# Conditioned graph attention: a re-ordered set-up, with batch 0's feature transform in seven block products

## The chip, the core and the metric

The kernel runs on one core of a Trainium2 chip. Its engines work in parallel, each through its own queue, in order: TensorE (PE in the profile, with its weight loads as PEld), VectorE (DVE), ScalarE (ACT), GpSimd (POOL) and SyncE (SP), which here only issues DMAs. They meet through semaphores. The metric is the device time of one execution in microseconds; lower is better. All arithmetic is float32 unless it is said otherwise.

## The reference

For 16 batches of 512 nodes with 512 features, a query vector is joined to every node (to nodes whose features sum to zero, a zero vector), and `self_feat = [x, q] @ W_self.T + b_self` follows. Twice, with an adjacency tensor and with its transposed form, 16-head attention over the first 20 nodes is added:

```python
vcq = concatenate([exp_v, where(row_zero, 0.0, q)], axis=-1)
self_feat = vcq @ W_self.T + b_self
output = self_feat
for d in range(2):
    A = (adj if d == 0 else swapaxes(adj, 1, 2))[:, :, :20, :]
    cond, vb = A.sum(-1), A @ w_bias + b_bias
    # heads of 32 features; keys and values are rows 0..19 of self_feat
    aff = einsum(q_heads, k_heads) / sqrt(32)
    aff = where(cond > 0, aff, -9e15) + vb
    output += grouped_output(softmax(aff) @ self_feat[:, :20])
return x + relu(output)
```

`x` is 16x512x512, the query 16x512, the label tensor 16x512x512x11 (int32), `W_self` 512x1024, and the query, key and output weights are two sets of 512x512.

## The kernel before, in words

Features lie on the 128 partitions in four chunks (C = 4) and nodes along the free dimension, halved and with the 20 key nodes put first in each half. A float32 matmul shows as two records in the trace. Several small matmuls run side by side in different parts of TensorE's array (`HA`, `HL` count such parts).

The work has two stages. The **set-up** is common to all batches; the **loop** does the 16 batches, software-pipelined over several periods, in an order written out by hand in the strings `order` and `moved`. The set-up too is issued in the order of the program text (`manual_schedule`), so that each engine's queue holds its instructions in that order.

The set-up goes through these steps:

- Loads of the 320 key-node columns (`xkv`), the feature half of `W_self` (`ws_v`) and the query half (`ws_q`), while seven warm-up matmuls run (L591).
- `kv_terms` (L646): the key nodes' features against `ws_v`, by chunk k of the contraction.
- The query's contribution `qw` (L656 to L671) and the flags `nzk` of key nodes with a non-zero sum (L663, L664); both are multiplied into `qp` (L681: one of the four by VectorE, three by GpSimd) and added into `kvT` (L686) and `kvn` (L690).
- `row_sums(0)` (L191, L193): GpSimd adds up batch 0's rows when `x` has landed, for the row flags. `row_flags` (L200, L203) counts with TensorE and stores the flags to DRAM, from where `load_nz` brings them back on all partitions.
- Eight `key_rows` (L703; copied out by L709 on ScalarE and L710 on VectorE), four of them ahead of the first burst and one ahead of each of bursts 1 to 4.
- Twenty bursts of `keys` (L800), n = 0 to 19: key rows against query weights, into two pairs of PSUM banks. ScalarE copies out one pair (L821) and VectorE the other (L823). The next burst writes the same banks. The finished groups go to DRAM (L826, four stage buffers).
- With bursts 0 to 3 VectorE also runs two `bias_terms` each (L719: a product of `wq_sb` and `br_sb`, both in SBUF, with an accumulated sum). From burst 4 on, the string `plan` names what else is issued behind each burst: `b` is `biases` (L725 to L731 on VectorE), `v` and `w` value matmuls (L769, copied out by L775, stored by L777), `n` and `l` the row flags and their loads, `c` the bias scores, `s` a step of batch 0's `self_feat`. At fixed bursts stand `weight_differences` (L787), the masks of batch 0 (`first_mask_mul`, `_count`, `_sum`: L337, L354, L357, L362) and, at burst 12, `weight_sums` (L241 to L244, GpSimd).

Batches 1 to 15 get their `self_feat` in the loop by seven block products of the 2x2 block matrices of weights and nodes, instead of eight (`feature_product`, L292). For that GpSimd forms sums of weight blocks once (`weight_sums`) and four differences of node blocks per batch (`x_sum`, L266). The products gather in two PSUM banks, `ps_u` and `ps_v`, and the copies in between (`feature_copy`, `feature_second`, `feature_third`, `feature_join`) add the query's part. Batch 0 is made directly: `self_feat` (L220), 16 matmuls for each of four blocks, three blocks in the set-up and the last at the entry of the loop, with `self_copy` (L232).

At the entry of the loop GpSimd forms sums of keys and features (`key_sum` L401, `self_sum` L411). The first of them writes memory that the set-up's pool held, so it waits for that pool's last users. The matmuls of the scores are L428 (`P1` to `P7`); `P6` needs `key_sum(0, 2)` and `self_sum(0, 2)`.

Of the kernel before, what the change touches and what calls it, by code (L numbers as in the profile page):

```python
# [8 lines left out]
I32 = mybir.dt.int32  # L9
AF = mybir.ActivationFunctionType  # L10
# [8 lines left out]
def gat_kernel(  # L19
# [68 lines left out]
    qw = const.tile([P, C, B], F32, name="qw")  # L88
# [4 lines left out]
    qd = const.tile([P, 2, B], F32, name="qd")  # L93
# [10 lines left out]
    wts, outs, held, sf_ps, conds, prods, both = {}, {}, [None] * 3, {}, {}, {}, {}  # L104
    sums, us, soft_w, diffs, held_sums = {}, {}, {}, {}, {}
# [105 lines left out]
    def self_feat(b, f, h, parts, to=None):  # L211

        for i, ks in parts:
            if (i, ks[0]) == (0, 0):
                if (f, h) == (0, 0):
                    new_self(b)
                held[0] = bank(f"ps_sf{b}_{f}{h}") if to is None else to
            for k in ks:
                for a in range(HA):
                    nc.tensor.matmul(  # L220
                        held[0][bass.ts(a, RA), bass.ds(i * HN, HN)],
                        ws_v[:, k, bass.ds((2 * f + i) * P + a * RA, RA)], xs[b][:, k, half(h)],
                        start=(i, k) == (0, 0), stop=k == C - 1, skip_group_check=True,
                    )
            if (i, ks[-1]) == (1, C - 1):
                sf_ps[b, f, h] = held[0]

    def self_copy(b, f, h):

        ps = sf_ps.pop((b, f, h))  # L230
        for i in range(2):
            nc.vector.scalar_tensor_tensor(  # L232
                sfs[b][:, 2 * f + i, half(h)], nzs[b][:, half(h)], qw[:, 2 * f + i, b : b + 1],
                ps[:, bass.ts(i, HN)], ALU.mult, ALU.add,
            )

# [20 lines left out]
    def x_sum(b, n):  # L257

        t = sums[b, n] = xsum.tile([P, 2, HN], F32, tag=f"t{n}", name=f"t{b}_{n}")
# [6 lines left out]
        nc.gpsimd.tensor_sub(t, one, two)  # L266

    def side(t):
        return t[:, : 2 * HN].rearrange("p (i n) -> p i n", i=2)

    def feature_product(b, n):
# [12 lines left out]
        for i in range(2):  # L284
            for k in range(2):
                for a in range(HA):
# [3 lines left out]
                    else:  # L290
# [3 lines left out]
                        start=(n, i, k) == (1, 0, 0), stop=k == 1, skip_group_check=True,  # L294
                    )

# [254 lines left out]
    with tc.tile_pool(name="setup", bufs=1) as sp, tc.tile_pool(  # L551
# [7 lines left out]
        sel = sp.tile([P, B], F32, name="sel")  # L559
# [12 lines left out]
        with tc.tile_pool(name="setup_k", bufs=1) as sk:  # L572
# [6 lines left out]
            nc.vector.memset(ps_q[:, 0], 0.0)  # L579
            nc.vector.memset(bqbd, 0.0)  # L580
            nc.gpsimd.memset(zero, 0.0)

            nc.gpsimd.memset(sel, 0.0)
            for k in range(C):
                nc.gpsimd.affine_select(
                    out=sel, in_=sel, pattern=[[-1, B]], compare_op=ALU.not_equal, fill=1.0,
                    base=-k * DH, channel_multiplier=1,
                )
# [22 lines left out]
            for k in range(3):  # L611
# [42 lines left out]

            for k in range(C):
                nc.tensor.matmul(  # L656
                    ps_q[bass.ds(k * DH, B), 0], q_sb[:, k], ws_q[:, k], start=True, stop=True
                )
            q4 = sk.tile([P, F], F32, name="q4")
            nc.scalar.copy(q4, ps_q[:, 0])  # L660
            ps = ps_s.tile([P, 2, 512], F32, tag="s", name="ps_q")
            counts = ps[:, 1, P : P + BM]
            nc.tensor.matmul(counts, ones, rsk, start=True, stop=True)  # L663
            nc.vector.tensor_scalar(nzk, counts, 0.0, None, ALU.not_equal)  # L664
            kv_terms(0, 3)
            for c in range(C):
                nc.tensor.matmul(
                    ps[:, c % 2, c // 2 * B : (c // 2 + 1) * B], q4[:, bass.ts(c, P)], sel,
                    start=True, stop=True,
                )  # L670
            nc.vector.tensor_copy(  # L671
                qw.rearrange("p (i a) b -> p a i b", a=2),
                ps[:, :, : 2 * B].rearrange("p a (i b) -> p a i b", b=B),
            )
            for fc in range(1, C):
                kv_terms(fc, 3)
            qps = []
            for fc in range(C):
# [4 lines left out]
                    qw[:, fc].unsqueeze(2).to_broadcast([P, B, NG]),  # L683
# [49 lines left out]
        with tc.tile_pool(name="setup_g", bufs=4) as sg:  # L733
# [94 lines left out]
            def self_step(b, f, h, i, k):  # L828
                self_feat(b, f, h, ((i, (k,)),), ps_v if (f, h) == (0, 1) else ps_u)
                if (i, k) == (1, C - 1):  # L830
                    self_copy(b, f, h)

# [13 lines left out]
            plan = "bvv nvv vv lccw vv ssss ssss vv vv ssss ssss vvn vv lww wsss sssss".split()  # L846
# [441 lines left out]
```

## Time and profile before

| | before |
|---|---|
| median of 3 runs | 550.07 us (548.75 to 550.30) |
| the profiled execution's own time | 549.49 us |
| its span | 547.6 us |
| mean granted TensorE clock | 0.996 |
| busy: PE, PEld, DVE, ACT, POOL | 99%, 76%, 83%, 67%, 78% |
| DMA | 122.90 MB, mean 224 GB/s |

Rows of the profile are in microseconds from the span's start. A time-ordered row gives start, duration, engine, line, operation, what it writes and reads, and how many instructions were merged; in square brackets stands how long the engine was idle ahead of it and what ended that. A row of the chain gives start, length, engine, tile and line. Matmuls overlap, so that their rows can overlap too; the chain gives each the part in which it set the pace.

### The profile page before, as it was taken

What the parts mean: (1) busy time and instruction counts of PE and PEld (TensorE: products, weight loads), DVE (VectorE), ACT (ScalarE), POOL (GpSimd) and SP (SyncE); (2) the same over time, 40 slices, a digit from 0 to 9 for tenths busy, and PEclk for the clock granted to TensorE, in tenths of its full rate; (3) what the DMA queues carried; (4) which work ended last, traced back from release to release, by engine and by line L of the source; (5) the groups of instructions that cost most, each with busy time, mean ns of one, the idle gap of its engine ahead of it and who ended that gap; (6) DMA issues with size and microseconds to landing.
All of it is one profiled execution on the core that took longest, in us unless ns stands there. A gap on an engine that the chain in (4) does not pass through costs nothing.

```text
span 547.6 us, 19531 instructions
## 1 busy us (share of the span) xinstructions
PE 540.1 (99%) x8126; PEld 416.1 (76%) x8126; DVE 455.0 (83%) x770; ACT 368.9 (67%) x803; POOL 426.2 (78%) x375
## 2 busy tenths in 40 slices
PE   9999999999999999999999999999999999999995
PEld 5444446989797979797878788887879797979794
DVE  1596663799989898989898998989898989898986
ACT  1145542868686959596868696868778686867554
POOL 2244413959797979797979899897979797979795
PEclk9999999999999999999999999999999999999998
DMA  8998979595685858676665657666657675745025
GB/s 302 388 416 324 351 286 362 184 302 167 219 260 172 256 176 238 199 218 224 195 231 174 227 186 218 218 196 211 204 193 242 190 253 179 224 132 166 23 79 193
DMA packets 87400, 122.90 MB, mean 224 GB/s; under 512 B 11656, under 2 KB 56208, under 8 KB 85264
## 3 DMA queue, kind: packets, MB, share of 16 engines
q1 hardware_dynamic: 86304, 120.47, 66.4%
q8 instruction: 64, 1.05, 0.8%
q10 hardware_dynamic: 1008, 1.19, 0.7%
q14 instruction: 24, 0.20, 0.1%
HBM read 84.99 MB, written 37.95 MB: 224 GB/s over the span
## 4 chain that ended last, share of the span: by engine, by line
PE 97%; DVE 1%; POOL 1%; ACT 0%; issue 0%; DVEq 0%; POOLq 0%
PE ps_a L428 23%; PE ps_u L292 18%; PE ps_v L292 14%; PE ps_e L428 11%; PE ps_w L428 6%; PE ps_w L520 6%; PE ps_v L769 3%; PE ps_k L703 2%; PE ps_a L994 2%; PE ps_u L220 1%; PE ps_v L220 1%; PE ps_e L520 1%; PE ps_kv L646 1%; PE ps_v L703 1%; PE ps_u L703 1%; PE ps_warm L591 1%
## 5 line engine op out<-in xcount | busy, mean ns | idle before, releaser
L492 POOL TENSOR_TENSOR s<-s,sm 128x640 f32<-128x640 f32 x60 | 76.4, 1276 | 40.3 <-DVE sm L488 40.2
L349 ACT ACTIVATE prod<-adj,wb_sb 128x160 f32<-128x160 int32 x165 | 80.5, 583 | 0.0
L545 POOL TENSOR_TENSOR o<-o,x 128x512 f32<-128x512 f32 x59 | 75.5, 1281 | 0.7 <-ACT o L1126 0.7
L483 ACT ACTIVATE s<-s 128x640 f32<-128x640 f32 x60 | 42.4, 730 | 25.7 <-DVE s L479 24.5
L292 PE MATMUL ps_u<-t,ws_s 128*64 128x246 f32 x480 | 55.0, 370 | 0.0
L456 DVE TENSOR_TENSOR u<-ps_a,both 128x640 f32<-128x640 f32 x30 | 24.7, 823 | 29.0 <-PE ps_a L428 29.0
L487 DVE TENSOR_REDUCE sm<-s 128x32 f32<-128x640 f32 x60 | 47.7, 795 | 0.0
L401 POOL TENSOR_TENSOR k<-g,k 128x608 f32<-128x608 f32 x30 | 43.9, 1482 | 1.1
L292 PEld LDWEIGHTS ps_u<-t,ws_s 128*64 128x64 f32 x480 | 33.9, 136 | 11.7
L411 POOL TENSOR_TENSOR s<-sf 128x512 f32<-128x512 f32 x30 | 37.8, 1278 | 6.2 <-DVE sf L322 5.3
L498 DVE STREAM_TRANSPOSE wt<-s 128x512 f32<-128x512 f32 x60 | 41.3, 689 | 0.2
L373 ACT COPY both<-add 64x160 f32<-64x160 f32 (+1 forms) x68 | 21.4, 315 | 23.7 <-DVE add L362 23.1
L266 POOL TENSOR_TENSOR t<-x 128x492 f32<-128x492 f32 x30 | 37.4, 1247 | 0.0
L520 PE MATMUL ps_w<-wt,vd 32*32 32x256 f32 (+1 forms) x600 | 36.6, 389 | 0.0
L520 PE MATMUL ps_e<-wt,vd 32*32 32x256 f32 (+1 forms) x600 | 36.6, 389 | 0.0
L401 POOL TENSOR_TENSOR k<-g 128x608 f32<-128x608 f32 x15 | 22.3, 1488 | 18.3 <-DMA vw_d<-v 17.6
L322 DVE TENSOR_TENSOR sf<-ps_v,f 128x492 f32<-128x492 f32 x45 | 30.0, 667 | 7.0 <-PE ps_v L292 6.2
L266 POOL TENSOR_TENSOR t<-x,t 128x492 f32<-128x492 f32 x30 | 34.6, 1153 | 0.2
L428 PEld LDWEIGHTS ps_a<-g,sf 128*64 128x64 f32 x480 | 30.3, 137 | 5.6 <-issue 5.4
L174 ACT ACTIVATE xn<-xn 128x512 f32<-128x512 f32 x56 | 34.5, 617 | 0.0
L362 DVE TENSOR_REDUCE add<-prod 128x160 f32<-128x1920 f32 (+1 forms) x17 | 34.5, 2028 | 0.0
L428 PE MATMUL ps_a<-g,sf 128*64 128x152 f32 x480 | 34.2, 295 | 0.0
(362 smaller groups left out, 1510.8 us busy)
## 6 DMA issues: line engine op xcount, KB each, us to landing
g_d<-st SPq DMA_DIRECT2D x16, 1064.0 KB
g<-g_d SPq DMA_DIRECT2D x56, 304.0 KB
out_T<-o SPq DMA_DIRECT2D x60, 256.0 KB
xn<-in_xn SPq DMA_DIRECT2D x28, 512.0 KB
x<-in_xT SPq DMA_DIRECT2D x28, 512.0 KB
adj<-in_adj SPq DMA_DIRECT2D x32, 440.0 KB
nz<-nz_d SPq DMA_DIRECT2D x16, 256.0 KB
vd<-bd_d SPq DMA_DIRECT2D x64, 64.0 KB
```

The lines of the kernel that those rows point to most:

```text
L266: nc.gpsimd.tensor_sub(t, one, two)
L292: nc.tensor.matmul(to[bass.ts(a, RA), bass.ts(i, HN)], lhs, x[:, k], start=(n, i, k) == (1, 0, 0), stop=k == 1, skip_group_check=True,)
L349: nc.scalar.activation(label_sums(b)[:, :, l], labels(b)[:, :, l], AF.Copy, scale=wb_sb[:, l : l + 1])
L401: op(t, one(), two())
L411: op(t, one(), two())
L428: nc.tensor.matmul(to[bass.ts(a, RA), j, :, 1:], rows[:, k, bass.ts(j, RA)], keys[:, k, a].rearrange("p (x m) -> p x m", m=ND), start=Fals ...
L483: nc.scalar.activation(t, t, AF.Exp)
L487: nc.vector.tensor_reduce(sm, rows_of(b, i, l), AX.X, ALU.add)
L492: nc.gpsimd.tensor_mul(t, t, us.pop((b, "sum", i, l)).unsqueeze(2).to_broadcast([P, 32, NG]))
L498: nc.vector.transpose(wts[b][:, i, l, : W * 4 // 5], t[:, :, :MW])
L520: nc.tensor.matmul((ps_w, ps_e)[a][to, g, bass.ts(c, NH)].rearrange("p (i j n) -> p i j n", i=2, n=32), lhs, rhs, start=False, stop=True, ...
L545: nc.gpsimd.tensor_add(t, t, xs[b][:, c])
```

## The change

- **Query.** The contraction over the 512 query features is accumulated in PSUM by 16 matmuls, four for each chunk, whose outputs are laid out so that one VectorE transposition of 32x32 blocks turns the result into `qw`. Before, four matmuls with 512 columns, a ScalarE copy, and four matmuls against a selection matrix did this; that matrix, built by four GpSimd selections, is gone. `qw` is padded to 32 columns.
- **Flags of the key nodes.** The column sums are counted by four matmuls of 80 columns on 32 output rows each; the flags are written as bfloat16, and four bfloat16 matmuls with a matrix of 1/32 spread them over all partitions. ScalarE copies the result to `nzk`.
- **Order.** The four `kv_terms` of the last chunk are issued together, behind this.
- **First weights.** Chunk 0 of `ws_v` comes in two loads of half the columns.
- **Batch 0.** Its `self_feat` is made by the seven block products, six in the set-up (the new plan letter `f`) and the last at the entry of the loop. Three copies `feature_early` put in the query's part, three `feature_join` finish blocks. The sums go into a buffer of the feature pool.
- **Positions.** `weight_sums` moves from burst 12 to burst 1; batch 0's four `x_sum` are new at bursts 2 and 3; the mask steps of batch 0, `row_sums(1)`, `row_flags(1)` and `load_nz(1)` move to earlier bursts.

The core of the diff:

```diff
-    qw = const.tile([P, C, B], F32, name="qw")
+    qw = const.tile([P, C, 32], F32, name="qw")
...
+    def place(b, kind, n):
+        if b:
+            return xsum.tile([P, 2, HN], F32, tag=f"{kind}{n}", name=f"{kind}{b}_{n}")
+        if kind not in early:
+            early[kind] = sfp.tile([P, C, N], F32, tag="sf", name=f"early_{kind}")
+        return side(early[kind][:, n - 1])
...
-    def feature_product(b, n):
+    def feature_product(b, n, starts=(1,), sides=range(2)):
...
-                        start=(n, i, k) == (1, 0, 0), stop=k == 1, skip_group_check=True,
+                        start=n in starts and (i, k) == (0, 0), stop=k == 1, skip_group_check=True,
...
+    def feature_early(n, f, l):
+        t = us[0, n] = place(0, "f", n)
+        for i in range(2):
+            nc.vector.scalar_tensor_tensor(
+                t[:, i], nzs[0][:, half(l)], qw[:, 2 * f + i, :1], ps_u[:, bass.ts(i, HN)], ALU.mult, ALU.add
+            )
...
-            nc.vector.memset(ps_q[:, 0], 0.0)
+            nc.vector.memset(ps_q[:, 0, :P], 0.0)
...
-            nc.gpsimd.memset(sel, 0.0)
-            for k in range(C):
-                nc.gpsimd.affine_select(
...
+            mean = sk.tile([P, HL, P], BF16, name="mean")
+            nc.gpsimd.memset(mean, 0.0)
+            for q in range(HL):
+                nc.gpsimd.memset(mean[bass.ts(q, 32), q], 1.0 / 32)
...
-            for k in range(3):
+            rows(xkv[:, :1], xkvT[:P])
+            for i in range(2):
+                nc.scalar.dma_start(ws_v[:, 0, bass.ts(i, HF)], wsT[:P, bass.ts(i, HF)])
+            for k in range(1, 3):
...
+            ps = ps_s.tile([P, 2, 512], F32, tag="s", name="ps_q")
+            BQ = BM // HL
+            for q in range(HL):
+                nc.tensor.matmul(
+                    ps[bass.ts(q, 32), 0, :BQ], ones[:, :32], rsk[:, bass.ts(q, BQ)], start=True, stop=True
+                )
+            flags = sk.tile([P, BQ], BF16, name="flags")
+            nc.vector.tensor_scalar(flags, ps[:, 0, :BQ], 0.0, None, ALU.not_equal)
             for k in range(C):
-                nc.tensor.matmul(
-                    ps_q[bass.ds(k * DH, B), 0], q_sb[:, k], ws_q[:, k], start=True, stop=True
-                )
-            q4 = sk.tile([P, F], F32, name="q4")
-            nc.scalar.copy(q4, ps_q[:, 0])
...
-            nc.tensor.matmul(counts, ones, rsk, start=True, stop=True)
-            nc.vector.tensor_scalar(nzk, counts, 0.0, None, ALU.not_equal)
-            kv_terms(0, 3)
-            for c in range(C):
-                nc.tensor.matmul(
-                    ps[:, c % 2, c // 2 * B : (c // 2 + 1) * B], q4[:, bass.ts(c, P)], sel,
...
-            for fc in range(1, C):
+                for a in range(HL):
+                    nc.tensor.matmul(
+                        ps_q[bass.ds(a * DH, B), 0, :P].rearrange("p (c x) -> p c x", x=DH), q_sb[:, k],
+                        ws_q[:, k].rearrange("p (c a x) -> p a c x", a=HL, x=DH)[:, a],
+                        start=(k == 0), stop=(k == C - 1),
+                    )
+            nc.vector.transpose(qw.rearrange("p c x -> p (c x)"), ps_q[:, 0, :P])
+            for q in range(HL):
+                nc.tensor.matmul(ps[:, 1, bass.ts(q, BQ)], mean[:, q], flags, start=True, stop=True)
+            nc.scalar.copy(nzk, ps[:, 1, :BM])
+            for fc in range(C):
                 kv_terms(fc, 3)
...
-            def self_step(b, f, h, i, k):
...
+            def features(n):
+                if n == 1:
+                    new_self(0)
+                feature_product(0, n, (1, 2, 5))
+                if n in (2, 3, 5):
+                    feature_join(0, *{2: (0, 0, 1), 5: (1, 1, 3), 3: (0, 1, 2)}[n])
+                else:
+                    feature_early(*{1: (1, 0, 0), 6: (2, 0, 1), 7: (3, 1, 1)}[n])
...
-                "s": [
-                    (self_step, (0, f, h, i, k)) for f, h in ((0, 0), (0, 1), (1, 1))
-                    for i in range(2) for k in range(C)
-                ],
+                "f": [(features, (n,)) for n in (1, 2, 6, 7, 5, 3)],
...
-            plan = "bvv nvv vv lccw vv ssss ssss vv vv ssss ssss vvn vv lww wsss sssss".split()
+            plan = "bvv nvv vv lccw vv f f nvv lvv f vv f vv ww fw f".split()
...
                 if rest:
                     for d in range(2):
                         bias_terms(d, (0, 2, 1, 3)[n])
+                    if n == 1:
+                        weight_sums()
+                    if n in (2, 3):
+                        for m in (2 * n - 3, 2 * n - 2):
+                            x_sum(0, m)
                     continue
...
+                if n == 4:
+                    first_mask_mul(0)
                 if n == 6:
-                    first_mask_mul(0)
+                    first_mask_count(0)
                 if n == 7:
-                    first_mask_count(0)
+                    first_mask_sum(0)
+                    row_sums(1)
...
-                if n == 12:
-                    weight_sums()
...
-        self_feat(0, 1, 0, ((0, range(C)),), ps_v)
+        feature_product(0, 4, (), (0,))
...
-        self_feat(0, 1, 0, ((1, range(C)),), ps_v)
-        self_copy(0, 1, 0)
+        feature_product(0, 4, (), (1,))
+        feature_third(0)
```

More of the change, by code (lines that the diff above doesn't have):

```diff
@@ L9 @@
 I32 = mybir.dt.int32
+BF16 = mybir.dt.bfloat16
 AF = mybir.ActivationFunctionType
@@ L92, in gat_kernel @@
     kvn = const.tile([P, C, BM], F32, name="kvn")
-    qd = const.tile([P, 2, B], F32, name="qd")
+    qd = const.tile([P, 2, 32], F32, name="qd")
     g01 = const.tile([P, 2, C * C, UW], F32, name="g01")
@@ L103, in gat_kernel @@
     xs, xns, rss, adjs, nzs, sfs, cqs, vds = {}, {}, {}, {}, {}, {}, {}, {}
-    wts, outs, held, sf_ps, conds, prods, both = {}, {}, [None] * 3, {}, {}, {}, {}
-    sums, us, soft_w, diffs, held_sums = {}, {}, {}, {}, {}
+    wts, outs, held, conds, prods, both = {}, {}, [None] * 3, {}, {}, {}
+    sums, us, soft_w, diffs, held_sums, early = {}, {}, {}, {}, {}, {}
     gs = {b: g01[:, b] for b in range(2)}
@@ L209, in half @@
         return slice(l * NH + NE, (l + 1) * NH)
[L211 to L223, printed above, removed]
-                    )
[L225 to L235, printed above, removed]
     def weight_sums():
@@ L257, in x_sum @@
     def x_sum(b, n):
-        t = sums[b, n] = xsum.tile([P, 2, HN], F32, tag=f"t{n}", name=f"t{b}_{n}")
+        t = sums[b, n] = place(b, "t", n)
         one, two = {
@@ L283, in feature_product @@
         to = ps_v if n in (2, 3, 5) else ps_u
-        for i in range(2):
+        for i in sides:
             for k in range(2):
@@ L558, in gat_kernel @@
         q_sb = sp.tile([P, C, B], F32, name="q_sb")
-        sel = sp.tile([P, B], F32, name="sel")
         bs_sb = sp.tile([P, C], F32, name="bs_sb")
@@ L682, in gat_kernel @@
                     qp, nzk.rearrange("p (b m) -> p b m", m=NG),
-                    qw[:, fc].unsqueeze(2).to_broadcast([P, B, NG]),
+                    qw[:, fc, :B].unsqueeze(2).to_broadcast([P, B, NG]),
                 )
@@ L826, in keys @@
                         nc.sync.dma_start(g_d[at_g], st)
-            def self_step(b, f, h, i, k):
-                self_feat(b, f, h, ((i, (k,)),), ps_v if (f, h) == (0, 1) else ps_u)
-                if (i, k) == (1, C - 1):
-                    self_copy(b, f, h)
+            def features(n):
[6 more added lines that the diff above has]
+                    feature_early(*{1: (1, 0, 0), 6: (2, 0, 1), 7: (3, 1, 1)}[n])
             steps = {
@@ L877, in gat_kernel @@
                     weight_differences(2 * n - 9)
+                if n == 4:
+                    first_mask_mul(0)
                 if n == 6:
-                    first_mask_mul(0)
+                    first_mask_count(0)
                 if n == 7:
-                    first_mask_count(0)
+                    first_mask_sum(0)
+                    row_sums(1)
+                if 7 < n < 10:
+                    mask_spread(0, (0,), (n - 8,))
                 if n == 9:
-                    first_mask_sum(0)
                     load_cq(0)
                 if n == 10:
-                    row_sums(1)
-                if n == 12:
-                    weight_sums()
-                if 9 < n < 12:
-                    mask_spread(0, (0,), (n - 10,))
-                if n == 13:
                     first_mask_mul(1)
+                if n == 11:
+                    first_mask_count(1)
                 if n == 14:
-                    first_mask_count(1)
-                if n == 15:
                     first_mask_sum(1)
-                if 15 < n < 18:
-                    mask_spread(0, (1,), (n - 16,))
+                if 14 < n < 17:
+                    mask_spread(0, (1,), (n - 15,))
     ps_loop = ctx.enter_context(tc.tile_pool(name="ps_loop", bufs=1, space=PSUM))
@@ L1140, in gat_kernel @@
         key_sum(0, 4)
-        self_feat(0, 1, 0, ((0, range(C)),), ps_v)
+        feature_product(0, 4, (), (0,))
         for n, t in enumerate(t[:, g] for t in (ps_a, ps_w, ps_e) for g in range(2)):
-            none = zero.bitcast(mybir.dt.bfloat16)[bass.ts(n % HL, 32), :P]
+            none = zero.bitcast(BF16)[bass.ts(n % HL, 32), :P]
             nc.tensor.matmul(
```

13 lines of the change are left out of this document (removed).

## The prediction

> **What bounds the kernel now.** I read the page first, then the chain of waits over the set-up (0 to 100 us, which is where every edit lies), then the time-ordered rows of each engine there.
>
> ```profile
> PE 540.1 (99%) x8126; PEld 416.1 (76%) x8126; DVE 455.0 (83%) x770; ACT 368.9 (67%) x803; POOL 426.2 (78%) x375
> PE 97%; DVE 1%; POOL 1%; ACT 0%; issue 0%; DVEq 0%; POOLq 0%
> ```
>
> TensorE (PE) carries 97% of the chain that ended last, and the loop after 100 us is untouched. So a microsecond gained or lost by PE before the loop should stay to the end. The chain in the two places where PE's own work changes:
>
> ```profile
> 1.03 3.35 PE ps_warm L591 x14
> 4.38 1.21 PE ps_kv L646 x16
> ...
> 10.98 0.86 PE ps_q L656 x8
> 11.84 0.74 PE ps_q L663 x2
> ...
> 13.25 1.03 PE ps_q L667 x8
> ...
> 16.04 2.38 PE ps_k L703 x32
> ...
> 42.30 0.36 PE ps_v L200 x8
> ...
> 90.03 1.81 PE ps_v L220 x16
> ...
> 93.91 1.66 PE ps_u L292 x16
> ...
> 95.60 2.29 PE ps_a L428 x32
> ```
>
> PE is never free, but another engine can stand just behind it. This view gives busy time by engine in three stretches, for PE, PEld, DVE, ACT and POOL in turn:
>
> ```profile
> 26.00:42.00 16.00, 16.00 (x336) 7.52 (x328) 15.55 (x47) 7.00 (x24) 7.08 (x5) 1.00 1.04 414
> 42.00:60.00 18.00, 18.00 (x373) 8.51 (x360) 12.78 (x33) 9.31 (x31) 11.26 (x10) 1.00 0.84 308
> 60.00:90.00 30.00, 29.54 (x488) 13.53 (x480) 18.10 (x46) 12.91 (x44) 3.07 (x3) 1.00 0.88 336
> ```
>
> From 26 to 42 us VectorE (DVE) works 15.55 of 16 us: it copies out each burst of `keys` matmuls, and PE may not start the next burst before that. GpSimd (POOL) is busy only 7.08 us there. The change puts ten microseconds more on POOL in just this stretch, so these rows decide:
>
> ```profile
> 26.33 1.29 POOL L191 TENSOR_TENSOR rx<-x 128x512 f32<-128x512 f32 x1 [9.09 <-DMA x<-in_xT]
> 27.69 3.30 POOL L193 TENSOR_TENSOR rx<-rx,x 128x512 f32<-128x512 f32 x2
> ...
> 52.72 2.64 POOL L193 TENSOR_TENSOR rx<-rx,x 128x512 f32<-128x512 f32 x2
> ```
>
> ```profile
> 27.26 0.90 DVE L719 SCALAR_TENSOR_TENSOR bqt<-wq_sb,br_sb 128x512 f32<-128x512 f32 x1
> ...
> 28.09 1.75 DVE L719 SCALAR_TENSOR_TENSOR bqt<-wq_sb,br_sb 128x512 f32<-128x512 f32 x1
> ...
> 29.78 0.53 DVE L710 SCALAR_TENSOR_TENSOR khD<-ps_k,bk_sb,kh 128x304 f32<-128x304 f32 x1
> ...
> 31.57 0.68 DVE L719 SCALAR_TENSOR_TENSOR bqt<-wq_sb,br_sb 128x512 f32<-128x512 f32 x1
> ...
> 32.18 0.68 DVE L719 SCALAR_TENSOR_TENSOR bqt<-wq_sb,br_sb 128x512 f32<-128x512 f32 x1
> ...
> 32.79 0.53 DVE L710 SCALAR_TENSOR_TENSOR khD<-ps_u,bk_sb,kh 128x304 f32<-128x304 f32 x1
> ...
> 40.82 0.16 DVE L725 TENSOR_TENSOR bqw<-bqw,bq_sb 128x8 f32<-128x8 f32 x1
> 41.02 0.70 DVE L727 TENSOR_SCALAR bqbd<-bqw 32x8 f32<-32x8 f32 x4
> 41.75 0.16 DVE L730 TENSOR_TENSOR bo<-bo_sb 128x4 f32<-128x4 f32 x1
> 41.95 0.16 DVE L731 TENSOR_TENSOR bo<-bo,bs_sb 128x4 f32<-128x4 f32 x1
> ```
>
> `bias_terms` (L719) is the same operation on two SBUF tensors each time. It takes 0.68 us where POOL is idle. The only two that meet POOL's row sums take 0.90 and 1.75. The first ends at 28.16, 0.54 after L191 ended (27.62); POOL's next operation then runs, and the second L719 ends at 29.84. The two row sums take 3.30 against 2.64 undisturbed. So the two engines take turns, a whole operation each. The copies from PSUM (L823, L710) keep their durations beside POOL.
>
> **Part 1: query and flags (10.98 to 18.42).** Out of PE go 0.86 (L656), 0.74 (L663) and 1.03 (L667). In come four flag matmuls of 80 columns (nearest row: L200, four of 128 columns, 0.36); the query in 16 matmuls of 128 columns instead of 4 of 512 (the same columns, 0.86); and four bfloat16 matmuls that spread the flags, which no row shows: between 0.1 and L667's 1.03, I take 0.5, since L667's four are float32 in two passes. PE's part falls from 2.63 to 1.72. What ends last there, however, is the flags and the query for POOL and DVE:
>
> ```profile
> 14.62 2.41 POOL L681 TENSOR_TENSOR qp<-nzk,qw 128x320 f32<-128x320 f32 x3 [5.95 <-DVE qw L671]
> 49.26 0.52 ACT L750 ACTIVATE c<-ps_u,bb_sb 128x304 f32<-128x304 f32 x1
> ```
>
> After the change: 10.98 + 0.36 + 0.86 + 0.50 = 12.70, then ScalarE's copy of the flags (L750's 0.52 and 0.06 to start) gives 13.28. The transposition runs beside it. POOL's `qp` starts there and not at 14.62: **-1.3** (from -1.8 to -0.8). All that follows, to the first burst, moves with it.
>
> **Part 2: first weights in two loads, other memsets.** Taken as 0. The warm-up matmuls hold PE to 4.38 and cover the load. Bounds: -0.2, and +0.46, which is one more issue on ScalarE's queue (1.38 for three) if it reached PE.
>
> ```profile
> 0.71 1.38 ACTq L594 DMA_DIRECT2D ws_v<-in_wsT  x3
> ```
>
> **Part 3: `weight_sums` and four `x_sum` put ahead of the plan, on POOL.** They now follow the row sums with nothing to wait for.
>
> ```profile
> 55.32 1.27 POOL L241 TENSOR_TENSOR ws_s<-ws_v 128x512 f32<-128x512 f32 x1
> L266 POOL TENSOR_TENSOR t<-x 128x492 f32<-128x492 f32 x30 | 37.4, 1247 | 0.0
> 47.60 2.10 POOL L337 TENSOR_TENSOR prod<-prod,wb_sb 128x880 f32<-128x880 f32 x1 [7.29 <-ACT prod L336]
> 35.80 1.29 POOL L787 TENSOR_TENSOR wq_sb<-wq_sb 128x512 f32<-128x512 f32 x1 [4.81 <-DVE bqt L719]
> ```
>
> POOL: 3 row sums (3.9), 4 x 1.27, 4 x 1.25 = 14.0 from 26.33, and some 0.55 for each turn given to DVE (seven): busy to about 44. Then `first_mask_mul` (L337, 2.10, moved up to here) and two `weight_differences` (L787, 1.29 each): to about 49. Every L719 of bursts 1 to 3 falls into this.
>
> A pair of L719 alone takes 32.79 - 31.57 = 1.22. Against a busy POOL: the rest of POOL's running operation (0 to 1.29, middle 0.64), 0.55 of its own, POOL's next operation (1.14 behind the DVE's end), 0.55: 2.88, or 1.66 more (1.0 to 2.3). Three pairs: **+5.0** (3.1 to 6.9). The pair of burst 0 already paid 29.78 - 27.26 - 1.22 = 1.30; 1.3 earlier its first one is done before x lands at 26.33 and its second still meets POOL: **-0.25** (to -1.3). DVE reaches L725 not at 40.82 but 40.82 - 1.3 - 0.25 + 5.0 = 44.3. PE came to burst 5 at 41.31, 0.49 behind the DVE, so it can lose that first: it starts at 44.3 + 0.1 for the hand-over, 3.1 late.
>
> ```profile
> 41.31 0.42 PE ps_g(4, 0, 0, 16)0_633 L800 x4
> ```
>
> Then `biases`: L725, L730 and L731 also read two SBUF tensors, while POOL has work to 49. Taken as 0.65 + 0.65 + 1.29 = 2.6 (0 if so small an operation slips through, to 2.1 + 1.29 + 1.29), less 0.3 of slack: **+2.3**. I take the wait because in the L719 rows it is POOL's remaining time, not the DVE operation's own length. PE is then 5.4 late at burst 6. From there on each burst gives DVE at most 2.8 us in 2.85, and PE sets the pace again.
>
> The Trainium skill ("SBUF — State Buffer", section "SBUF: two separate sides") says the same more generally: the pair of ports shared by the two engines is "an exclusive lock, not a bandwidth split", held for the whole instruction, by a VectorE operation with two SBUF inputs against a GpSimd one that reads SBUF. By it, 0.90 and 1.75 are waits (the trace agrees), and the three small ones wait as well; were only the 128x512 ones hit, the sum would be 2.3 less, 552.2. The page counts VectorE's 2-port modes too; if L727 runs in one, up to one POOL operation (1.29) would come on top, 555.8, which no row shows.
>
> **Part 4: batch 0 by seven products.** In the set-up 6 products of 8 matmuls stand for 48 matmuls: no change (1.66 in L292's row, 1.81 in L220's, each for 16 records, two a matmul). The flags of batch 1 move up by four bursts (0.36 out, 0.36 in, L200). With them SP's queue gets their load one burst behind their store, not two, and waits for the landing; behind it stand a value store and a key store. Three spare stage buffers of 1.25 bursts each (2.85 us a burst) hide that: 0. On DVE three `self_copy` become three `feature_early` and three `feature_join`, 2.0 us more in a stretch where it has 12 free (60 to 90): 0, and 2.0 if that cover were gone. Behind burst 19, `feature_product(0, 4)` has 8 matmuls where `self_feat` had 16: PE has 1.66 less to do before 95.60. But what ends there?
>
> ```profile
> 91.49 1.48 POOL L401 TENSOR_TENSOR k<-g 128x608 f32<-128x608 f32 x1 [17.63 <-DMA vw_d<-v]
> 92.92 1.28 POOL L411 TENSOR_TENSOR s<-sf 128x512 f32<-128x512 f32 x1
> 94.28 1.27 POOL L411 TENSOR_TENSOR s<-s,sf 128x512 f32<-128x512 f32 x1
> ```
>
> PE's `P6` at 95.60 needs the sum that ends at 95.55, and that chain began when the last value store landed. A PE that comes 1.66 sooner waits there. The store moves only by what leaves the DMA queue ahead of it, the load of batch 1's row flags (256 KB, some 0.65 us at that stretch's 336 to 414 GB/s): **-0.4** (0 to -1.66).
>
> **Sum** against the profiled execution's 549.49 (span 547.6 and 1.9 around it; the median of the runs is 550.07, 0.58 above): -1.3 - 0.25 + 5.0 - 0.35 (PE's slack, with the hand-over) + 2.3 - 0.4 = +5.0, **554.5 us**.
>
> **Rivals.** A difference under 0.3% (1.65 us) can hardly be told here from none.
>
> *Faster: POOL and DVE do not collide, or rarely.* Six of the eight L719 in the traces took 0.68; if POOL's new work left the DVE alone, -1.3 - 0.4, and 0.4 of what burst 0's pair costs today: **547.4**. Against it: both rows that met POOL. It decides from where the pairs and `biases` cost less than some 2 us together.
>
> *About even: the lower bounds hold.* Pairs at 3.1, `biases` slip through: -1.3 - 0.25 + 3.1 - 0.35 - 0.4 = +0.8, **550.3**.
>
> *The seven products save nothing* (P6's wait eats all): +0.4, **554.9**; inside the forecast, and likely.
>
> *Worse: the upper bounds.* Pairs +6.9, small operations +4.4: **558.5**.
>
> **How the numbers follow.** Forecast 0.68 (its own range 551.5 to 557.5: pairs and small operations between their bounds, query -1.8 to -0.8); faster 0.20; even 0.07; worse 0.05. The range reaches down to 547.5, into the faster case, and leaves out about 0.16. Slower 0.73, same 0.07, faster 0.20.
>
> **What would show it.** The L719 rows of bursts 1 to 3 above 1.2 us on average, POOL without a gap from 26 to 45, burst 5 (`4, 0, 0`) starting near 44.4, and L725, L730, L731 above 0.16; `qp` on POOL at 13.3; `P6` waiting for POOL. It is wrong if L719 stays at 0.68, or if PE keeps its bursts gapless while DVE is late.

## The result and the profile after

The changed kernel takes 556.33 us, the median of five runs (553.74 to 557.41), against 550.30 for the kernel before: a ratio of 1.0108, with a 95% interval from 1.0076 to 1.0139. It is slower by about 6 us; 554.5 was forecast. The profiled execution took 556.33 us (span 554.5), 6.84 more than the profiled 549.49 of before. Three executions of the later sessions (621.6, 700.0 and 1964.1 us) fell far outside the rest and are in no ratio; the first is the profiled one of run 1, whose rows below are therefore those of its repeat.

The page after, its busy line and the chain's shares by engine:

```profile
PE 541.3 (98%) x8136; PEld 416.0 (75%) x8136; DVE 464.5 (84%) x773; ACT 368.9 (67%) x803; POOL 434.0 (78%) x379
PE 87%; DVE 4%; DMA 4%; POOL 1%; issue 1%; SPq 1%; ACT 0%; ACTq 0%; DVEq 0%; POOLq 0%
```

TensorE works hardly longer in all (541.3 us against 540.1) in a span 6.9 us longer, so nearly all of the difference is waiting. Its share of the chain fell by more than that, from 97% to 87%, because the chain now reaches TensorE for the first time at 51.25 us and runs over loads and VectorE before. What TensorE itself lost shows in the stretches of the set-up. Busy time by engine in the same three stretches as before (PE, PEld, DVE, ACT, POOL; then granted clock, DMA share, GB/s):

```profile
26.00:42.00 16.00, 14.13 (x292) 7.05 (x287) 15.93 (x35) 6.06 (x22) 14.03 (x10) 1.00 1.00 390
42.00:60.00 18.00, 14.80 (x247) 6.01 (x248) 14.52 (x30) 6.18 (x19) 11.19 (x10) 0.91 0.55 220
60.00:90.00 30.00, 28.77 (x528) 13.01 (x528) 21.17 (x53) 14.64 (x50) 3.14 (x3) 1.00 0.86 319
```

GpSimd's 7.08 us in the first stretch became 14.03; TensorE lost 1.87 us of its 16 there, 3.2 of 18 in the next, and the granted clock fell to 0.91. GpSimd's rows and VectorE's, in order of time:

```profile
27.66 1.49 POOL L192 TENSOR_TENSOR rx<-x 128x512 f32<-128x512 f32 x1 [10.28 <-DMA x<-in_xT]
...
36.75 1.74 POOL L219 TENSOR_TENSOR ws_s<-ws_v,ws_s 128x512 f32<-128x512 f32 x1
...
46.55 2.51 POOL L777 TENSOR_TENSOR wq_sb<-wq_sb 128x512 f32<-128x512 f32 x2
```

```profile
31.42 1.32 DVE L709 SCALAR_TENSOR_TENSOR bqt<-wq_sb,br_sb 128x512 f32<-128x512 f32 x1
...
32.67 1.76 DVE L709 SCALAR_TENSOR_TENSOR bqt<-wq_sb,br_sb 128x512 f32<-128x512 f32 x1
...
45.14 1.48 DVE L715 TENSOR_TENSOR bqw<-bqw,bq_sb 128x8 f32<-128x8 f32 x1
46.66 2.80 DVE L717 TENSOR_SCALAR bqbd<-bqw 32x8 f32<-32x8 f32 x4
49.49 0.16 DVE L720 TENSOR_TENSOR bo<-bo_sb 128x4 f32<-128x4 f32 x1
```

L709 is the old L719 (`bias_terms`), L715 to L721 are `biases`. GpSimd has no gap from 27.66 to 49.06. In it a `bias_terms` pair takes 2.7 to 3.0 us, the 128x8 addition 1.48 (0.16 before), and the four 32x8 scalings 2.80 (0.70 before). Only what comes after 49.06 is back at its old 0.16.

### The profile page after: what moved, and what is told of

It reads as the page before. It is cut to its first block, busy times and chain, and to the rows that moved or that the text cites. A ratio compares the mean times of both kernels' runs of the same rounds, so it can differ in the third digit from the quotient of the medians.

```text
span 554.5 us, 19557 instructions
## 1 busy us (share of the span) xinstructions
PE 541.3 (98%) x8136; PEld 416.0 (75%) x8136; DVE 464.5 (84%) x773; ACT 368.9 (67%) x803; POOL 434.0 (78%) x379
## 4 chain that ended last, share of the span: by engine, by line
PE 87%; DVE 4%; DMA 4%; POOL 1%; issue 1%; SPq 1%; ACT 0%; ACTq 0%; DVEq 0%; POOLq 0%
PE ps_a L419 22%; PE ps_u L275 19%; PE ps_v L275 14%; PE ps_e L419 11%; PE ps_w L419 6%; PE ps_w L511 6%; PE ps_v L759 3%; PE ps_a L987 2%; DMA wq_sb<-in_wq 1%; DVE bqt L709 1%; DMA bq_sb<-in_bq 1%; DVE st L813 1%; DMA ws_v<-in_wsT 1%; PE ps_e L511 1%; DMA vw_d<-v 1%
## 5 line engine op out<-in xcount | busy, mean ns | idle before, releaser
L345 DVE TENSOR_REDUCE cond<-adj 128x160 f32<-128x1760 int32 (+1 forms) x17 | 31.1, 1829 | 4.4 <-DMA adj<-in_adj 4.4
```

## The experiments

All times are medians; a ratio is to the kernel before in the same session (550.8 to 551.0 us there), with its 95% interval. Differences to the changed kernel are to its 556.3 us, which two sessions gave (run 5); the kernel before moved by 0.7 us between sessions, so they are good to about that.

**1. The sums later.** The weight sums, the x sums and the first mask product go behind `bias_terms` and `biases`; all else of the change stays.

```diff
-                    if n == 1:
-                        weight_sums()
-                    if n in (2, 3):
-                        for m in (2 * n - 3, 2 * n - 2):
-                            x_sum(0, m)
...
-                if n == 4:
-                    first_mask_mul(0)
                 if n == 6:
+                    first_mask_mul(0)
                     first_mask_count(0)
                 if n == 7:
                     first_mask_sum(0)
                     row_sums(1)
+                    weight_sums()
+                    for m in range(1, 5):
+                        x_sum(0, m)
```

> The changed kernel, with the weight sums, the four x sums and the first mask product no longer ahead of the plan on GpSimd: the mask product goes back to burst 6, the sums stand behind batch 1's row sums at burst 7. All else of the change stays. Theory (GpSimd and VectorE take turns on SBUF): the six bias_terms operations of bursts 1 to 3 take 0.68 us again, three pairs 3.7 us instead of 8.6; the row of four small scalings (32x8) falls from 2.80 to 0.70 us and the 128x8 addition from 1.48 to 0.16; no TensorE wait before burst 6, and TensorE does not slow down behind it (the 16 value matmuls there 1.9 us, not 2.8). Time 547 to 550 us. Rival (the loss comes from the loads, the query part or the seven products): bias_terms gets shorter, but the time stays above 554. At the loop entry P6 should now wait about 1 us for GpSimd, since its last store lands when the DMA queue lets it.

Measured: 549.54 us, ratio 0.9978 (0.9956 to 1.0000). The same kernel once more, in a later session:

> The kernel with the late sums alone, first weights in two loads, once more, next to kernels with one load on the same chip. Theory (the second load makes SyncE's queue wait, x lands about 1.1 us later, and the row sums then meet more of bias_terms): 1 to 2 us slower than the kernel with late sums and one load, which was 3.0 us under the kernel before. Rival (part 2 costs nothing): within 0.5 us of it.

Measured: 548.77, ratio 0.9960 (0.9939 to 0.9981). Its rows (the trace of the later run):

```profile
32.01 0.67 DVE L709 SCALAR_TENSOR_TENSOR bqt<-wq_sb,br_sb 128x512 f32<-128x512 f32 x1
...
41.80 0.16 DVE L715 TENSOR_TENSOR bqw<-bqw,bq_sb 128x8 f32<-128x8 f32 x1
41.99 0.70 DVE L717 TENSOR_SCALAR bqbd<-bqw 32x8 f32<-32x8 f32 x4
```

Placing alone accounts for the whole loss: with the sums later, the change is 1 to 2 us faster than the kernel before. Two expectations missed by a little: `P6` waits 0.3 us for GpSimd, not 1, and TensorE waits 0.3 us at burst 2, where no wait was expected.

**2. One SBUF input.** GpSimd's queue stays as the change has it; `bias_terms` reads one SBUF tensor.

```diff
-                nc.vector.scalar_tensor_tensor(
-                    t, wq_sb[:, d, c], 1.0, br_sb, ALU.mult, ALU.mult, accum_out=bqw[:, d, c : c + 1],
-                )
+                nc.vector.tensor_reduce(bqw[:, d, c : c + 1], wq_sb[:, d, c], AX.X, ALU.add)
```

> The changed kernel with its GpSimd queue as it is, but each bias_terms operation on VectorE reads one SBUF tensor instead of two: a sum over wq_sb (tensor_reduce) in the place of the product with br_sb and its sum. That leaves the factor br_sb out of the bias, so the output is not the reference's. Theory (only an operation with two SBUF inputs excludes GpSimd): each of the eight takes about 0.6 us (from the mask count's 1.05 for 880 elements) in all bursts, with GpSimd just as busy; VectorE reaches the biases about 5 us sooner, near 40 us; the biases still meet GpSimd's mask product and weight differences and still cost 3 to 5 us. Time 550 to 552.5. Rival (any VectorE operation on SBUF is slowed beside a busy GpSimd): they take 1.1 to 1.8 us and the time stays near 556.

Measured: 552.02 us, ratio 1.0011 (0.9994 to 1.0029). VectorE (each first row is a pair of two operations), and the end of GpSimd's stretch:

```profile
33.81 1.27 DVE L708 TENSOR_REDUCE bqw<-wq_sb 128x1 f32<-128x512 f32 x2
...
40.65 1.01 DVE L712 TENSOR_TENSOR bqw<-bqw,bq_sb 128x8 f32<-128x8 f32 x1
41.70 4.66 DVE L714 TENSOR_SCALAR bqbd<-bqw 32x8 f32<-32x8 f32 x4
```

```profile
43.64 2.50 POOL L774 TENSOR_TENSOR wq_sb<-wq_sb 128x512 f32<-128x512 f32 x2
```

Beside a GpSimd that is just as busy, the reduction takes 0.64 us each, in every burst, and GpSimd's own operations are back at 1.28. So it is not SBUF traffic as such. The reduction also writes 128x1 where `bias_terms` wrote 128x512, so this run alone does not tell the second input from the larger output. And the theory as I had put it, that only two SBUF inputs exclude GpSimd, fell: the 32x8 scalings have one input and take longer still, 4.66 us for 0.70. `biases` ends at 46.75, 0.6 behind GpSimd. (Of the 4.3 us under the changed kernel, the traces put 1.2 down to a pause of TensorE at 73 us that is missing here; more on that below.)

**3. `biases` later.** The changed kernel, `biases` at burst 6 in place of burst 4.

```diff
-            plan = "bvv nvv vv lccw vv f f nvv lvv f vv f vv ww fw f".split()
+            plan = "vv nvv bvv lccw vv f f nvv lvv f vv f vv ww fw f".split()
```

> The changed kernel with one thing moved: biases (the 128x8 addition, four 32x8 scalings, two 128x4 additions on VectorE) stands in burst 6 of the plan, not in burst 4, so that GpSimd's mask product and weight differences should be over (49.1 us in the changed kernel). Theory (the small operations wait for GpSimd too, 3.3 us in all, and the 2.4 us that TensorE then waits slows it down for another 1 us): the seven operations take 0.16 to 0.18 each, VectorE's copy of burst 5 starts near 45.3, not 49.8, TensorE has no half-speed stretch at 53 us, and the time falls by 3 to 4.5 us, to 552 to 553.5. Rival (the pairs alone made TensorE late, and the small operations stood in time that was lost anyway): the time falls by less than 1 us.

Measured: 552.52 us, ratio 1.0021 (1.0001 to 1.0042), 3.8 under the changed kernel:

```profile
48.81 0.16 DVE L715 TENSOR_TENSOR bqw<-bqw,bq_sb 128x8 f32<-128x8 f32 x1
49.01 0.71 DVE L717 TENSOR_SCALAR bqbd<-bqw 32x8 f32<-32x8 f32 x4
```

The same small operations, 0.7 us behind GpSimd's end (48.06 here), take what they took before, and TensorE's granted clock stays at 1.00 from 44 to 56 us. Seven operations of 1.3 us in all cost, with what followed from them, some 4 of the 6 us.

**4. The weight sums alone, in the kernel before.**

```diff
                         bias_terms(d, (0, 2, 1, 3)[n])
+                    if n == 1:
+                        weight_sums()
...
-                if n == 12:
-                    weight_sums()
```

> The kernel before with one part of the change alone: the four weight sums on GpSimd at burst 1, not at burst 12 (no x sums, no moved mask product). Theory: GpSimd is busy from 26.3 to about 37 us without a gap, so the bias_terms pairs of bursts 1 and 2 take 2.9 us each, not 1.22: VectorE comes 3.4 us later to the biases, which are not hit, since GpSimd has nothing else then; 0.5 of it is covered. Time 552 to 553.5. Rival (nothing of the loss comes from this): 549.5 to 550.5. It also shows a second head of the kernel before: at what time TensorE goes from 0.53 to 0.27 us for four 320-column weight changes (before: already at 4.3 us; changed kernel: 7.1).

Measured: 552.58 us, ratio 1.0023 (1.0004 to 1.0043).

```profile
27.52 1.75 DVE L719 SCALAR_TENSOR_TENSOR bqt<-wq_sb,br_sb 128x512 f32<-128x512 f32 x1
...
32.69 1.29 DVE L719 SCALAR_TENSOR_TENSOR bqt<-wq_sb,br_sb 128x512 f32<-128x512 f32 x1
...
33.91 1.76 DVE L719 SCALAR_TENSOR_TENSOR bqt<-wq_sb,br_sb 128x512 f32<-128x512 f32 x1
...
37.23 0.68 DVE L719 SCALAR_TENSOR_TENSOR bqt<-wq_sb,br_sb 128x512 f32<-128x512 f32 x1
```

GpSimd is busy to 36.8; the pairs before that (bursts 0 and 1, not 1 and 2 as expected) cost 3.4 and 2.9 us, those behind it 1.2. TensorE is 2.4 late from burst 4 on. This one move makes the kernel slower, by 1.3 us (0.2 to 2.4).

**5. The changed kernel again**, nothing edited.

> The changed kernel once more, nothing edited. Time 5 to 7 us above the kernel before. Theory (when TensorE reaches full speed in the first microseconds is chance, not the change): the time at which four 320-column weight changes go from 0.53 to 0.27 us apart will not be 7.1 again but somewhere from 4.3 to 7.7 us, and the first burst's copy moves with it, by up to 1.4 us, while the pairs of bias_terms in bursts 1 to 3 sum to 8.4 to 8.8 us and the biases to 4 to 6 as before. Rival (the split load or the later landings hold TensorE back): again 7.1.

Measured: 556.28 us, ratio 1.0100 (1.0083 to 1.0117). The first value matmuls in the profiles of the changed kernel, of this run, and of the kernel before:

```profile
4.33 2.36 PE L637 MATMUL ps_kv<-xkv,ws_v 128*32 128x320 f32 x16
```

```profile
4.33 1.50 PE L637 MATMUL ps_kv<-xkv,ws_v 128*32 128x320 f32 x16
```

```profile
4.31 1.28 PE L646 MATMUL ps_kv<-xkv,ws_v 128*32 128x320 f32 x16
```

The same program does these 16 in 2.36 us once and in 1.50 the next time, so the change does not slow them. TensorE starts at half speed, and when it reaches the full one varies: sets of four of its weight loads, all of one shape, start 0.53 us apart in the first of these profiles (5.40, 5.93, 6.46) and 0.27 apart at the same place in the second (5.39, 5.66, 5.93). The first burst starts at 23.88 here, 1.0 sooner than in the first profile (24.88). Yet the time is the same, since GpSimd's stretch ends late all the same:

```profile
43.12 0.62 DVE L715 TENSOR_TENSOR bqw<-bqw,bq_sb 128x8 f32<-128x8 f32 x1
43.77 4.66 DVE L717 TENSOR_SCALAR bqbd<-bqw 32x8 f32<-32x8 f32 x4
```

```profile
45.73 2.48 POOL L777 TENSOR_TENSOR wq_sb<-wq_sb 128x512 f32<-128x512 f32 x2
```

VectorE came to `biases` 2 us sooner than in the first profile, and left it 1 us sooner: 48.8, again 0.6 behind GpSimd's 48.2. The pairs of bursts 1 to 3 sum to 8.2 us, a little under the 8.4 to 8.8 expected. What is gained ahead is mostly waited for there.

**6. One load, and the query part.** Three kernels in the session of run 5, all with the late sums: the first weights in one load, the same with the old query and flags, and the same with the last value step ahead of the product step.

```diff
-            rows(xkv[:, :1], xkvT[:P])
-            for i in range(2):
-                nc.scalar.dma_start(ws_v[:, 0, bass.ts(i, HF)], wsT[:P, bass.ts(i, HF)])
-            for k in range(1, 3):
+            for k in range(3):
```

> The kernel with the late sums (they stand at burst 7, the mask product at burst 6), and the first 128 rows of ws_v again in one load on ScalarE's queue, not two. Theory (part 2 costs nothing, since nothing that SyncE's queue brings later is waited for): SyncE's wait for ws_v to land falls from 3.6 us to about 1, x lands near 26.3 us and not 27.7, and the time is that of the late sums alone, within 0.5 us: about 1.5 us under the kernel before. Rival (the later landings cost what the query part gained): another 1 us or more is gained, 2.5 us under the kernel before.

Measured: 547.76 us, ratio 0.9945 (0.9927 to 0.9963).

> The kernel with the late sums and one first load, and with the query and the key flags computed as in the kernel before (512-column query, selection matrix, flags by 128x320 matmuls): what is left of the change is batch 0's seven products and the order of the mask steps. Theory (the query part gains 1.3 us that reach the end): 1.0 to 1.6 us slower than the kernel with late sums and one load. Rival (that gain is lost before the first burst's copy): within 0.5 us of it.

Measured: 548.34 us, ratio 0.9960 (0.9946 to 0.9973).

```diff
-            plan = "bvv nvv vv lccw vv f f nvv lvv f vv f vv ww fw f".split()
+            plan = "bvv nvv vv lccw vv f f nvv lvv f vv f vv ww wf f".split()
```

> The kernel with the late sums and one first load, and in the plan of burst 18 the last value step ahead of the product step, so that its store is issued some 1.8 us sooner. Theory (with seven products POOL's chain at the loop's entry follows this store, and TensorE's P6 waits for it 0.2 to 0.3 us): P6 waits no more, 0.2 to 0.3 us gained, hardly to be measured. Rival (P6 waits over 1 us when TensorE is not late before it): 1 us or more gained against the kernel with late sums and one load.

Measured: 548.26 us, ratio 0.9959 (0.9945 to 0.9972). The value step's place makes no difference that can be measured: `P6` waits 0.6 us there, not less. One load came out 3.0 us under the kernel before, nearer to the rival's 2.5 than to the theory's 1.5. The repeat of run 1 was to settle that, and does not: with two loads it is 0.8 us behind by the ratios (0.9960 against 0.9945), with overlapping intervals. SyncE does wait longer for `ws_v` with two loads (2.4 to 3.7 us against 0.8 to 1.3). `x` lands at 26.8 us in both of the profiles compared, but over all profiles in which GpSimd starts with it, it lands at 26.8 to 27.8 with two loads and at 26.1 to 26.8 with one. The run with the old query has one load and late sums, so what it keeps of the change is the seven products and the order: these are worth 2.2 us (0.9960). And the new query is worth 0.6 us between the medians, with overlapping intervals, where 1.0 to 1.6 was expected. The rows of burst 0 with the new query, and with the old one, show why:

```profile
27.35 1.25 DVE L706 SCALAR_TENSOR_TENSOR bqt<-wq_sb,br_sb 128x512 f32<-128x512 f32 x1
...
28.52 1.75 DVE L706 SCALAR_TENSOR_TENSOR bqt<-wq_sb,br_sb 128x512 f32<-128x512 f32 x1
```

```profile
27.92 0.68 DVE L710 SCALAR_TENSOR_TENSOR bqt<-wq_sb,br_sb 128x512 f32<-128x512 f32 x1
...
28.53 1.76 DVE L710 SCALAR_TENSOR_TENSOR bqt<-wq_sb,br_sb 128x512 f32<-128x512 f32 x1
```

Batch 0's row sums on GpSimd run from `x`'s landing (26.8 and 26.6) to about 31. The sooner VectorE comes, the more of its pair falls into them: the first burst starts 0.57 sooner with the new query, burst 5 0.54 later (42.22 against 41.68).

**7. The row sums later too**, behind `bias_terms`, with the new query and with the old one; the plan then has `biases` at burst 7 and the row flags two bursts later.

```diff
-            row_sums(0)
...
+                if n == 6:
+                    weight_differences(3)
+                    row_sums(0)
...
-            plan = "bvv nvv vv lccw vv f f nvv lvv f vv f vv ww fw f".split()
+            plan = "vv vv nvv lbvv ccw f f nvv lvv f vv f vv ww fw f".split()
```

> The kernel with late sums and one first load, and with batch 0's row sums on GpSimd also behind VectorE's bias_terms: they stand after the second weight difference, the row flags two bursts later, the biases at burst 7, the first mask copy at burst 5. Theory (the query part's 1.3 us are there at the first burst but go back to VectorE's wait for the row sums, whose start is set by x landing, not by the query): all eight bias_terms operations take 0.68 us, burst 5 starts 0.8 to 1.3 us sooner than in the kernel with late sums and one load, and the time is 0.5 to 1.3 us lower, 3 to 4.5 us under the kernel before. Rival (something else holds bursts 1 to 4, or the biases meet GpSimd at their new place): no gain or a loss of up to 2 us.

Measured: 552.18 us, ratio 1.0021 (1.0008 to 1.0034).

> The kernel with late sums, one load and late row sums, with the query and the key flags as in the kernel before. Theory (with no operation of VectorE waiting for GpSimd, the query part's gain reaches the end): 1.0 to 1.3 us slower than the kernel with the new query. Rival (it is lost elsewhere): within 0.4 us of it.

Measured: 553.95 us, ratio 1.0055 (1.0033 to 1.0078).

With nothing on GpSimd beside `bias_terms`, all eight take 0.68 or 0.69, and burst 5 starts 1.16 us sooner (41.06 against 42.22), as the theory had it. The query part is worth 1.8 us between these two medians, 1.0 in the traces at each burst and at `P6`. But the rival holds for the time: at their new place `biases` met the row sums of batch 1.

```profile
49.39 0.42 DVE L712 TENSOR_TENSOR bqw<-bqw,bq_sb 128x8 f32<-128x8 f32 x1
49.85 2.68 DVE L714 TENSOR_SCALAR bqbd<-bqw 32x8 f32<-32x8 f32 x4
52.56 1.19 DVE L717 TENSOR_TENSOR bo<-bo_sb 128x4 f32<-128x4 f32 x1
```

```profile
48.52 1.28 POOL L192 TENSOR_TENSOR rx<-x 128x512 f32<-128x512 f32 x1
49.87 2.62 POOL L194 TENSOR_TENSOR rx<-rx,x 128x512 f32<-128x512 f32 x2
```

4.6 us for what takes 1.3: the same collision, moved to another burst. It is not the whole loss: behind waits of 1.64 and 1.95 us TensorE's granted clock is at half from 58.4 to 61.8 us, and `P6` waits 1.3 us for GpSimd. The lowest median stays that of late sums with one load, 0.55% under the kernel before; run 1's repeat and the two other kernels of run 6 overlap it.

**8. One load in the changed kernel.** The edit of run 6's first diff, on the changed kernel.

> The changed kernel with one thing undone: the first 128 rows of ws_v in one load. Theory (GpSimd's stretch without a gap starts when x lands, and VectorE gets through the biases only when that stretch ends): x lands about 1 us sooner, GpSimd's second weight difference and the biases end about 1 us sooner, and the time falls by 0.7 to 1.3 us. Rival (the landing of x doesn't matter there): within 0.4 us of the changed kernel.

Measured: 555.22 us, ratio 1.0081 (1.0061 to 1.0101), 1.1 under the changed kernel in size as expected, but the intervals overlap. GpSimd's stretch starts at 26.37 and ends at 48.45, against 48.2 and 49.1 in the two profiles with two loads. It also has a gap of 1.07 us ahead of the mask product, which waits there for ScalarE, so that the sooner start is partly lost. This one is not settled.

## Why the prediction was right or wrong

The forecast was slower by 5.0 us; the profiled executions differ by 6.84, the medians by 6.0. The cause it named is the cause: runs 1, 2 and 4 show it from three sides. That the sum came out so near is partly luck: errors of both signs met in it. Of its rivals, "the upper bounds" (558.5) is nearly as close to the measured time as the forecast; in the rows the pairs cost their middle value and the small operations 3.4, between 2.6 and that rival's 4.4.

| Step | Predicted | In the profile of after |
|---|---|---|
| VectorE at `biases` | 44.3 (+3.5) | 45.14 (+4.3) |
| `biases`, small operations | +2.6 | +3.4 |
| TensorE's slack up to burst 6 | -0.65 | -0.8 |
| TensorE at half speed behind its wait | none | +1.7 |
| Bursts 7 to 19 | 0 | +0.5 |
| Loop's entry, seven products | -0.4 | -1.9 |
| The loop | 0 | -0.3 |
| Sum (of the unrounded rows) | +5.0 | +6.8 |

The first two rows are 45.14 against 40.82, and 49.85 - 45.14 against 1.29; the rest are differences between the starts of the same burst (or of `P6`) in the two traces.

**Part 1, query and flags (-1.3): the step was right, that it moves on to the end was not.** The first row is of before, the other two of after:

```profile
10.79 1.04 PE L656 MATMUL ps_q<-ws_q,q_sb 128*16 128x512 f32 x8
```

```profile
12.18 0.31 PE L649 MATMUL ps_q<-rsk,ones 128*32 128x80 f32 x8
```

```profile
14.69 2.41 POOL L671 TENSOR_TENSOR qp<-nzk,qw 128x320 f32<-128x320 f32 x3 [5.46 <-ACT nzk L664]
```

From TensorE's flag matmuls to GpSimd's `qp` it takes 2.51 us now (12.18 to 14.69), against 3.83 from the same point before (10.79 to 14.62): 1.3 gone. `qp` still starts at 14.69 and not at 13.28, since in this execution TensorE came 1.4 us later to that point, by the half speed of run 5 (there `qp` starts at 13.70). The prediction let the gain pass to the end. Runs 5, 6 and 7 show that it passes only where no VectorE operation has to wait for GpSimd; otherwise the wait takes it or most of it, for GpSimd starts when `x` lands.

**Part 2, first weights in two loads (0):** open. It looked at ScalarE's queue and at TensorE alone, not at SyncE's, where the wait for `ws_v` grew from 1.0 to 3.7 us; `x` landed at 27.66, not 26.33, and GpSimd's stretch began so much later. What that cost is not settled: one load gains 0.8 us in run 6 and 1.1 in run 8, both with overlapping intervals.

**Part 3, the pairs (+5.0, and -0.25 for burst 0): right, by mechanism and size.** Bursts 1 to 3 in one row (shortest, median, longest of six, in ns):

```profile
L709 DVE SCALAR_TENSOR_TENSOR bqt<-wq_sb,br_sb x6: 1129/1534/1759, 31.4 to 41.8; 128x512 f32<-128x512 f32 x6
```

The pairs take 2.94, 2.97 and 2.71 from the first one's start to the next operation's, 8.6 in all against 3.7: +5.0. Burst 0's pair takes 2.30, 0.2 less than before, as forecast, but by luck: VectorE came to it no sooner (27.32 against 27.26), it was `x` that landed 1.3 later.

**Part 3, the small operations (+2.6): mis-sized, and by the term that I had put aside.** Waits were given to L725, L730 and L731 and none to the scalings L727 (now L717). In the profile the last two did not wait, GpSimd being done; the scalings took 2.10 longer. The prediction had this as the Trainium skill's case of a 2-port mode ("SBUF — State Buffer", "SBUF: two separate sides"), which no row showed then. Now 2.80, 4.66 and 4.66 us for four operations of 0.17 show the wait, in line with that rule, though no run shows the mode itself; the reduction of run 2, one input and no wait, is its other side. There is a simpler estimate than a sum of single waits: in the four profiles in which `biases` meets the stretch of the changed kernel (runs 2, 5, 8 and the first), it ends 0.6 to 0.8 us behind GpSimd's last operation. With seven operations against the three or four that GpSimd has left, the stretch's end sets it, whether VectorE arrives at 40.65 (run 2) or at 45.14.

**What no step had: TensorE slows down behind a long wait.** The rows around burst 6, before and after, and the clock of after:

```profile
44.33 0.34 PE L800 MATMUL ps_g(4, 1, 9, 16)1_679<-khD,wq_sb 32*64 32x133 f32 x4
...
45.33 1.92 PE L769 MATMUL ps_v<-wo_sb,kvT 128*32 128x512 f32 x16
```

```profile
51.25 0.34 PE L790 MATMUL ps_g(4, 1, 9, 16)1_699<-khD,wq_sb 32*64 32x133 f32 x4 [2.40 <-DVE g L813]
...
52.97 2.86 PE L759 MATMUL ps_v<-wo_sb,kvT 128*32 128x512 f32 x16
```

```profile
52.90:56.00 3.10, 3.10 (x35) 0.83 (x32) 2.42 (x6) 1.25 (x5) 0.34 (x1) 0.67 0.81 298
```

Sixteen value matmuls take 2.86 here and 1.93 at 59.79, and the part of burst 6 ahead of them 1.72 instead of 1.00. TensorE is 6.9 late at 51.25 and 8.6 late at burst 7 (55.76 against 47.19). In the trace the granted clock is 0.50 from 51.5 to 54.9 us and 1.00 on both sides.

**Part 4, the seven products (-0.4): mis-sized.** From the start of the last burst to `P6` it took 11.07 us before (84.53 to 95.60) and 9.21 now (93.57 to 102.78): -1.9, beyond the bound of -1.66. It is 9.1 to 9.6 in the other kernels with seven products, except run 7's two (10.3), and 11.4 in run 4, without them. `P6` does wait for GpSimd, but little:

```profile
102.78 2.29 PE L419 MATMUL ps_a<-k,s 128*64 128x152 f32 x32 [0.24 <-POOL s L402]
```

The step that failed is "the store moves only by what leaves the DMA queue ahead of it", which I priced at 0.65: GpSimd's chain starts 5.10 us behind that burst's start (98.67), not 6.96, and 2.9 us after the last value store was issued where it had been 4.6. It does follow the store's landing, by 0.4 us in both traces. Whether the moved load or the store's later place in the plan did that was not separated; issuing the store sooner (run 6) brought nothing.

**The 0.5 us of bursts 7 to 19** are pauses of TensorE of up to 1.2 us that the profile puts down to no other engine. The kernel before has them too, at other places; three of the kernels here (runs 2 and 7) have none. What they are stays open.

**The rivals.** "POOL and DVE do not collide" fell with every row of L709; its price was good, though: it said 547.4, and the kernels that were built without the collision at bursts 1 to 4 take 547.8 to 549.5. "The seven products save nothing" fell with the 1.9 us of the loop's entry.

## What to carry to other kernels

Before work is moved to an idle engine, list what the engines that share something with it do in that stretch, the very small operations too: here seven operations of 1.3 us in all took 4.7, because three of them each waited for a whole operation of the neighbour. Price such a meeting by turns, one operation of the neighbour for each that has to wait, until one side has none left. Where the neighbour runs out first, the stretch's end sets the time, and what is gained ahead of it is waited away. After a move that failed, look at where the same operations will meet next.

## What the runs showed of the hardware that was not expected

TensorE's first microseconds differ from run to run of one program. Busy time in the same 2.8 us, before and after:

```profile
4.30:7.10 2.80, 2.80 (x45) 1.40 (x48) 0.00 (x0) 1.28 (x1) 1.11 (x2) 1.00 1.05 353
```

```profile
4.30:7.10 2.80, 2.80 (x25) 1.10 (x28) 0.00 (x0) 0.00 (x0) 0.86 (x1) 1.00 0.91 302
```

25 matmuls instead of 45, and the column of the granted clock says 1.00 for both. The trace's record of the clock only begins at 4.24 us in the first and at 7.13 in the second, and what lies ahead of it counts as 1.00; the durations of the matmuls show the half speed. In thirteen profiles those first sixteen took from 1.28 to 2.36 us and the record begins at 4.24 to 7.20, in the same order and whatever was edited. Among the kernels with the new query the first burst moves with it by up to 1.2 us. The Trainium skill ("TensorE: Matmul & The Clock Gate", Part 1) has a gate that looks at activity in windows of some 3.4 us which do not begin with the kernel; that agrees in kind, though the spread seen here is wider than the half microsecond to both sides that the page states. Later in the kernel the clock column does show it. In the set-up five profiles have a stretch at 0.50, of 3.4 us (the changed kernel, both of run 7) or 6.8 us (runs 2 and 5). In the 3.4 us just before it TensorE was busy for 0.10 to 0.47 of the time; in run 8, with 0.50 in such a stretch, the clock stayed at 1.00. One long wait is not needed: 2.40 us was the longest in the changed kernel, 1.95 in run 7. The full clock came back after 3.4 us where TensorE was busy for 0.96 of them or more, and only after 6.8 where it was busy for 0.70 or 0.85 of the first half. These are few cases, and at the kernel's very end the clock also falls behind stretches with more than 0.50, so no threshold follows from them.

The other surprise is how small an operation can be and still lose a whole turn: a 32x8 scaling of 0.17 us takes up to 2.03 beside GpSimd (run 2), while a 128x512 reduction of 0.64 passes GpSimd freely.
